# Attention values of one batch by seven products of blocks, in halves of the TensorE array's columns

## The chip, the cores and the metric

The program runs on one core of a Trainium2 chip. The core has five engines that run their own instruction streams and meet through semaphores: TensorE (matrix products, in the profile PE, and PEld for the loading of the stationary operand), VectorE (DVE), ScalarE (ACT), GpSimd (POOL) and SyncE (SP, which here issues the DMAs). The metric is the device time of one execution in microseconds (us), less is better. Three runs of the kernel before took 2408.09 to 2408.88 us, with a median of 2408.5 us.

## What is computed

The input is four images `x` of 512 channels and 32 x 32 places (1024 tokens), float32. Four layers follow each other, each adding its result to `x`: attention with eight heads of 64 channels, a linear attention, attention with one head of 512 channels after a layer norm, and attention with four heads of 128 channels after a group norm. The change is in the last layer, of which this is the core:

```python
attn = jnp.einsum('bhdn,bhdm->bhnm', q, k) / math.sqrt(hd)   # hd = 128, 4 heads
attn = jax.nn.softmax(attn, axis=-1)
out = jnp.einsum('bhnm,bhdm->bhnd', attn, v)
...
return x + conv1x1(out, proj_w, proj_b)
```

## The kernel before

Images are worked off one after another. For each, `project_qkv` makes queries, keys and values, and `attention` (from L917) does the rest. All data are float32, and a float32 matmul shows as two matmul instructions in the trace, each with a weight load of its own.

In the four-head layer a *step* `(qb, g, i)` is one block of 512 queries (`qb`, two of them), one head (`g`, four) and two tiles of 128 keys (`i`, four): 32 steps for an image. Step n of the last image is meant by its number from 0 to 31, so steps 0 to 3 are head (0,0), steps 12 to 15 head (0,3), steps 28 to 31 head (1,3).

- `scores(n)`: two matmuls with a full 128x128 stationary operand and 512 moving columns (L953), into a PSUM tile of two banks, of which there are two. One exponential on ScalarE over 128x1024 (L958) writes the tile `pt`, of which there are four. VectorE keeps the running sum of the head's exponentials (L964 for the second step of a head, L967 after that) and at the head's last step adds the two halves of the sum (L974).
- `values(n)`: two matmuls (L999) that multiply the values of the step's keys with `pt` and add up in one PSUM bank `acc` over the four steps of a head. There are four such banks. At the head's last step ScalarE copies the result to a part of the tile `ot` (L1007); there is one such tile, so the first head of the second query block waits with its copy until the first block has been projected.
- `sum_shared` (L1035): sums over the keys for all heads of a query block in one PSUM bank, with a stationary operand of 128x32 per head; then the reciprocal on VectorE (L693) and two maxima over it that a range check needs (L696), and a round trip by DMA through HBM that spreads the quotients over the partitions (L1047, L1050). In the last image the last head is left out of its block's sharing and has a sum of its own, `sum_rows` (L1024).
- `normalise` (L1068): VectorE multiplies `ot` with the quotients, three ticks after the sums, `issue_after` the newest running sum.
- `project_out` (four ticks after the sums): the output projection of the first block, by seven products of blocks (L1095), with the additions on VectorE (L1103, L1126). It stands in TensorE's stream as one piece of about 12 us.
- `end_program`: for the last query block of the last image; full products (L1146), of which three quarters are done before the last head is normalised, then the result of the range check (L1746 to L1751), the rest, and the output DMAs.

The loop at the end of `attention` writes the order down: iteration m does `scores(m)`, then for step m - 2 the sums if it is a head's last step, and `values(m - 2)`, then a tick for what is due later. TensorE's stream is kept in just this order (a manual schedule). The other engines' instructions are ordered by the framework's scheduler by readiness and priority; `soon()` raises the priority of an exponential, `issue_after` puts an instruction behind a named one.

"Seven products" is a scheme that other parts of the kernel use already: a product of 2 x 2 blocks by seven block products in place of eight, with four sums of weight blocks (`sum_weights`, on GpSimd, L711 to L715) and four sums of input blocks (`sum_inputs`, L701 to L704). Two places use a stationary operand of 64 columns, one in each half of the array's columns: `features(1)` of the linear attention (L1404) and `keys_times_values` (L1529), which also swaps the two halves of the partitions by two DMAs (L1537).

Of the kernel before, what the change touches and what calls it, by code (L numbers as in the profile page):

```python
# [13 lines left out]
F32 = mybir.dt.float32  # L14
AF = mybir.ActivationFunctionType
ALU = mybir.AluOpType
AX = mybir.AxisListType

P = 128
# [3 lines left out]
NC = C // P  # L23
NT = S // P
TB = 512
# [450 lines left out]
def plain_path(ctx: ExitStack, tc: tile.TileContext, d: dict, out: bass.AP, count):  # L476
# [11 lines left out]
    nc = tc.nc  # L488
# [11 lines left out]
    def acc_tile():  # L500
        return ps_acc.tile([P, TB], F32, tag="acc", name="acc")
# [7 lines left out]
    def pt_tile(name):  # L509
        return work.tile([P, 2, TB], F32, tag="pt", bufs=4, name=name)  # L510
# [15 lines left out]
    def chunks_tile(tag, name, bufs=1):  # L526
        return work.tile([P, NC, TB], F32, tag=tag, bufs=bufs, name=name)
# [389 lines left out]
    def attention(b, q, key, v, heads, scale, wo, os, bo, hooks={}, last=False, end=None):  # L917
# [7 lines left out]
        x = xs[b]  # L925
# [14 lines left out]
        group_of = {u: us for us in shared for u in us}  # L940
        parts_of, adds = {}, []

        def scores(n):
            qb, g, i = steps[n]
            ps = two_tile("sc")
            if pair:
                for h, s in itertools.product(range(2), range(2)):
                    nc.tensor.matmul(  # L948
                        ps[half(h), s, :], lhsT=key(g, i)[half(s), half(h)],
                        rhs=q[qb][half(s), g, :], start=True, stop=True,  # L950
                    )
            for s in range(0 if pair else 2):
                nc.tensor.matmul(  # L953
                    ps[:, s, :], lhsT=key(g, 2 * i + s), rhs=q[qb][:, g, :], start=True, stop=True
                )
            pt = pt_tile("pt")
            with soon():
                exps.append(nc.scalar.activation(pt, ps, AF.Exp, scale=scale).ins)  # L958
            pts[n] = pt
            us = group_of.get((qb, g), [])  # L960
            if i == 1:
                acc = many_tile("sum")[:, :2, :] if pair and g % 2 and us else sum_tile("sum")
                accs[qb, g] = acc
                adds.append(nc.vector.tensor_tensor(acc, pts[n - 1], pt, ALU.add).ins)  # L964
            elif i > 1:
                acc = accs[qb, g]
                adds.append(nc.vector.tensor_tensor(acc, acc, pt, ALU.add).ins)  # L967
            if i == nsteps - 1 and not pair:
                total = acc[:, 0, :]
                if us:  # L970
                    if g == 0:
                        parts_of[qb] = many_tile("sums")
                    total = accs[qb, g] = parts_of[qb][:, g, :]
                nc.vector.tensor_tensor(total, acc[:, 0, :], acc[:, 1, :], ALU.add)  # L974

        def values(n):
            qb, g, i = steps[n]
            pt = pts.pop(n)
            if i == 0:
                outs[qb, g] = [acc_tile() for _ in range(2 if pair else 1)]  # L980
# [189 lines left out]

        per = 2 if pair else 1
        parts = []
        for m in range(0, len(steps) + 2, per):
            for n in range(m, m + per):
                if n < len(steps):
                    scores(n)
            for n in range(m, m + per):
                if n >= 2:
                    qb, g, i = steps[n - 2]
                    final = i == nsteps - 1  # L1180

                    us = group_of.get((qb, g))
# [2 lines left out]
                        sum_shared(us)  # L1185
                    elif final and not pair and not us:
                        sum_rows(qb, g)
                    values(n - 2)
                    tick()
                    if final and pair and closes:  # L1190
                        if n - 2 < len(steps) - 1:
                            later.append([1, lambda us=us: sum_shared(us)])
                        else:
                            sum_shared(us)
# [4 lines left out]
                        later.append([3, lambda us=us: normalise_shared(us)])  # L1199
                    elif final and not pair and not us:  # L1200
                        normalise(qb, g)
                    if n - 2 == len(steps) - 1 and end is not None:
                        flush()
                        end_program(qb)
                    elif final and g == NC - 1:
# [828 lines left out]
```

## Time and profile before

The profiled execution took 2407.96 us by the device's clock; the profile's own span is 2406.2 us, the rest lies around it.

| what | us | from |
|---|---|---|
| span | 2406.2 | page |
| profiled execution | 2407.96 | times |
| TensorE matmul busy | 2396.1 | page, part 1 |
| four-head layer, scores (all images) | 239.8 | L953, 512 instructions |
| four-head layer, values (all images) | 240.8 | L999, 512 instructions |
| first scores of the last image start | 2261.13 | timeline |
| first row sums, after the scores of step 17 | 2317.87 | timeline, L1035 |
| `project_out` of the first block | 2334.42 to 2346.5 | timeline, L1095 |
| second row sums | 2372.35 | timeline, L1035 |
| `end_program` starts | 2386.32 | timeline, L1146 |

How to read it: a busy time is the union of an engine's instructions, so two that run side by side count once; the mean is that of one instruction from its start to its end, and on TensorE it holds the way through the array, so matmuls overlap (one of 512 columns lasts 0.59 us and the next starts 0.43 us after it). A weight load starts when the matmul before its own starts. In the timeline an entry in brackets is the time that the engine was idle before the instruction, and what ended it.

### The profile page before, as it was taken

Reading aid. Unit: us, or ns where it says so; the run is one execution under the profiler, and the core shown is the slowest. Engines: PE = TensorE matmul, PEld = TensorE weight load, DVE = VectorE, ACT = ScalarE, POOL = GpSimd, SP = SyncE. Lnnn points to the kernel's source line nnn. Section 1 sums busy time; section 2 is a strip of 40 time slices with the busy share of each in tenths; the row PEclk is TensorE's granted clock in tenths of the full one; section 3 lists DMA queues with packets and bytes.
Section 4 is the critical chain, followed back from the end, with each engine's and each line's share of the span. In section 5 each row is a group of like instructions: output and inputs, shape, how many; then the busy total and the mean of one; then the engine's idle time right before and its main releaser. Section 6 shows DMA issues by size and latency. Waiting matters only on the chain. (4 is left out here: it accounts for less than half of the span.)

```text
span 2406.2 us, 24706 instructions
## 1 busy us (share of the span) xinstructions
PE 2396.1 (100%) x10014; PEld 1197.0 (50%) x10014; DVE 1505.6 (63%) x1834; ACT 702.1 (29%) x866; POOL 245.9 (10%) x240
## 2 busy tenths in 40 slices
PE   9999999999999999999999999999999999999999
PEld 5444544453445344544646445455556446455653
DVE  3678577757875789685585865654563554445344
ACT  1454154315531653230302202013321330331132
POOL 4001100110020001102102021011020001002000
PEclk9999999999999999999999999999999999999999
DMA  6001220212021213111002020110010001000001
GB/s 188 10 10 36 57 80 10 62 31 80 19 62 63 100 37 95 64 66 79 18 9 79 22 87 0 62 70 18 36 70 1 22 31 53 0 35 36 0 25 43
DMA packets 45895, 112.28 MB, mean 47 GB/s; under 512 B 3807, under 2 KB 21215, under 8 KB 42830
## 3 DMA queue, kind: packets, MB, share of 16 engines
q1 hardware_dynamic: 45774, 110.64, 13.7%
q8 instruction: 80, 1.31, 0.2%
q14 instruction: 41, 0.34, 0.0%
HBM read 75.79 MB, written 33.78 MB: 46 GB/s over the span
## 5 line engine op out<-in xcount | busy, mean ns | idle before, releaser
L958 ACT ACTIVATE pt<-sc 128x1024 f32<-128x1024 f32 x384 | 379.6, 1022 | 531.4 <-PE sc L953 303.9
L967 DVE TENSOR_TENSOR sum<-sum,pt 128x1024 f32<-128x1024 f32 x256 | 314.5, 1229 | 160.8 <-ACT pt L958 147.5
L984 PE MATMUL acc<-pt,v 64*64 64x512 f32 x2048 | 245.7, 591 | 0.0
L948 PE MATMUL sc<-q,k 64*64 64x512 f32 x2048 | 243.8, 591 | 1.1 <-ACT pt L958 1.1
L999 PE MATMUL acc<-pt,v 128*128 128x512 f32 x512 | 240.8, 594 | 0.0
L953 PE MATMUL sc<-q,k 128*128 128x512 f32 x512 | 239.8, 593 | 0.0
L724 PE MATMUL acc<-t,ws 128*128 128x512 f32 x384 | 173.9, 593 | 0.0
L711 POOL TENSOR_TENSOR ws<-wqkv 128x256 f32<-128x256 f32 (+1 forms) x40 | 39.2, 981 | 1289.9 <-PE acc L1035 513.3
L964 DVE TENSOR_TENSOR sum<-pt 128x1024 f32<-128x1024 f32 x64 | 78.0, 1219 | 137.0 <-ACT pt L958 137.0
L999 PEld LDWEIGHTS acc<-pt,v 128*128 128x128 f32 x512 | 96.6, 190 | 125.3 <-issue 121.6
L953 PEld LDWEIGHTS sc<-q,k 128*128 128x128 f32 x512 | 96.8, 190 | 116.2 <-issue 92.9
L984 PEld LDWEIGHTS acc<-pt,v 64*64 64x64 f32 x2048 | 76.8, 133 | 143.9 <-issue 141.5
L948 PEld LDWEIGHTS sc<-q,k 64*64 64x64 f32 x2048 | 76.4, 133 | 141.8 <-issue 132.9
L724 PEld LDWEIGHTS acc<-t,ws 128*128 128x128 f32 x384 | 72.7, 190 | 88.1 <-issue 86.3
L763 ACT COPY v<-acc 128x512 f32<-128x512 f32 x24 | 14.1, 586 | 305.1 <-PE acc L849 305.1
L693 DVE RECIPROCAL rd<-acc 128x512 f32<-128x512 f32 (+1 forms) x25 | 83.8, 3353 | 29.1 <-PE acc L1035 29.1
L763 ACT COPY q<-acc 128x512 f32<-128x512 f32 x40 | 23.4, 586 | 221.1 <-PE acc L724 221.1
L849 PE MATMUL acc<-ws,t 128*128 128x256 f32 x384 | 87.1, 380 | 0.0
L1095 PE MATMUL acc<-ot,wo 128*128 128x256 f32 x360 | 85.4, 382 | 1.7 <-DVE ot L1068 1.7
L856 PE MATMUL acc<-q,ln 128*128 128x512 f32 x192 | 86.6, 594 | 0.0
L856 PE MATMUL acc<-qs,w 128*128 128x512 f32 x192 | 86.5, 592 | 0.0
L754 DVE TENSOR_TENSOR v<-acc,v 128x512 f32<-128x512 f32 x72 | 49.7, 690 | 53.1 <-PE acc L849 53.0
(321 smaller groups left out, 3392.6 us busy)
## 6 DMA issues: line engine op xcount, KB each, us to landing
home<-x SPq DMA_DIRECT2D x8, 2048.0 KB
x<-home SPq DMA_DIRECT2D x8, 2048.0 KB
rds<-quotients SPq DMA_DIRECT2D x32, 256.0 KB
squares<-squares SPq DMA_DIRECT2D x32, 256.0 KB
out<-x SPq DMA_DIRECT2D x31, 256.0 KB
rds<-quotients SPq DMA_DIRECT2D x7, 1024.0 KB
x<-in_x SPq DMA_DIRECT2D x3, 2048.0 KB
v<-squares SPq DMA_DIRECT2D x12, 512.0 KB
```

The costliest lines, as they stand in the source:

```text
L693: nc.vector.reciprocal(rd, ps)
L724: nc.tensor.matmul(ps, lhsT=w[:, m, :], rhs=x[:, m, :], start=start, stop=stop, skip_group_check=True)
L849: nc.tensor.matmul(ps[:, bass.ts(r, C // 2)], lhsT=x[:, m, bass.ts(2 * o + r, P)], rhs=w[:, m, :], start=(start and r == 0), stop=stop, sk ...
L856: nc.tensor.matmul(ps, lhsT=x[:, m, bass.ts(o, P)], rhs=w[:, m, :], start=start, stop=stop, skip_group_check=True,)
L948: nc.tensor.matmul(ps[half(h), s, :], lhsT=key(g, i)[half(s), half(h)], rhs=q[qb][half(s), g, :], start=True, stop=True,)
L953: nc.tensor.matmul(ps[:, s, :], lhsT=key(g, 2 * i + s), rhs=q[qb][:, g, :], start=True, stop=True)
L958: exps.append(nc.scalar.activation(pt, ps, AF.Exp, scale=scale).ins)
L964: adds.append(nc.vector.tensor_tensor(acc, pts[n - 1], pt, ALU.add).ins)
L967: adds.append(nc.vector.tensor_tensor(acc, acc, pt, ALU.add).ins)
L984: nc.tensor.matmul(outs[qb, g][r][half(s), :], lhsT=v[i // 2][half(r), i % 2, g * P + s * hd : g * P + (s + 1) * hd], rhs=pt[half(r), s, : ...
L999: nc.tensor.matmul(outs[qb, g][0], lhsT=v[j // 2][:, j % 2, bass.ts(g, P)], rhs=pt[:, s, :], start=(j == 0), stop=(j == NT - 1),)
L1095: nc.tensor.matmul(ps[i][:, bass.ts(o, n)], lhsT=w[:, m, bass.ts(o, P)], rhs=t[:, m, :], start=(start and m + o == 0), stop=(stop and m == ...
```

## The change

In the last image alone, for the six heads between the first and the last, the product of values and exponentials is done by seven products of blocks. The blocks of a pair of steps: output, 2 x 2 blocks of 64 channels by 256 queries; inner, two blocks of 256 keys (one step each). A block product has a stationary operand of 128x64 and 256 moving columns and is written to one half of PSUM's partitions, that is to one half of the array's columns. The products are listed in two rows, `left` and `right`, and issued in turn, one of each: four turns at the first step of a pair, three at the second.

- The sums of value blocks (`vsums`) are made once at the start, eight GpSimd instructions of 128x512. The sums of exponentials (`sum_keys`) are made for each pair of steps: three subtractions of 128x512 on GpSimd (the second needs the first, the third the second), one (t[2]) on VectorE.
- A head has two accumulators. Since products for one output block land in different halves, `seven_values` ends a head with two ScalarE copies (`own` in the new tile `room`, and `ot`), two DMAs that swap the halves of `own`, and five VectorE additions, `issue_after` the newest running sum.
- Exponentials go to a ring of six (`ring`, in the storage of the projection's weights), and values follow their scores by three iterations (`lag`), not two.

```diff
+        lag, ring, by_seven = 2, None, set()
+        if end is not None:
+            lag, by_seven = 3, {(qb, g) for qb, g, i in steps[nsteps:-nsteps:nsteps]}
+            ring = wpool.tile([P, 6, 2, TB], F32, tag="wqkv", name="pts")
+            vsums = [chunks_tile("xn", "vs", 2) for _ in range(2)]
+            for kh in range(2):
+                blocks = [
+                    t.rearrange("p m (g i c) -> p (m g) i c", g=NC, i=2)
+                    for t in v[2 * kh : 2 * kh + 2]
+                ]
+                sum_weights(
+                    [vsums[kh][:, k, :].rearrange("p (r c) -> p r c", r=2 * NC) for k in range(4)],
+                    lambda i, j: blocks[j][:, :, i, :],
+                )
+            room = xpool.tile([P, 2 * NC, TB], F32, tag="x", bufs=2, name="room")
+            tsums = {}
+
+        def sum_keys(n):
+            ts = [pt_tile("t") for _ in range(2)]
+            t = [ts[k // 2][:, k % 2, :].rearrange("p (m q) -> p m q", m=2) for k in range(4)]
+            inputs = lambda j, tb: pts[n - 1 + j][:, :, bass.ts(tb, TB // 2)]
+            nc.gpsimd.tensor_tensor(t[0], inputs(0, 1), inputs(0, 0), ALU.subtract)
+            nc.gpsimd.tensor_tensor(t[1], inputs(1, 1), t[0], ALU.subtract)
+            nc.vector.tensor_tensor(t[2], inputs(1, 1), inputs(0, 1), ALU.subtract)
+            nc.gpsimd.tensor_tensor(t[3], inputs(1, 0), t[1], ALU.subtract)
+            tsums[n - 1] = t
+
+        def seven_values(n):
...
+            left = [(0, 0, raw(0, 0, m), inp(0, 0, m), m == 0, m == 1) for m in range(2)]
+            left += [(1, 0, raw(0, 1, m), inp(1, 0, m), m == 0, m == 1) for m in range(2)]
+            left += [(1, 1, sm(3, m), inp(1, 1, m), False, m == 1) for m in range(2)]
+            left += [(0, 1, sm(0, 0), t[0][:, 0, :], False, True)]
+            right = [(0, 1, sm(0, 1), t[0][:, 1, :], True, True)]
+            right += [(0, 0, sm(1, m), t[1][:, m, :], False, m == 1) for m in range(2)]
+            right += [(1, 1, sm(2, m), t[2][:, m, :], m == 0, m == 1) for m in range(2)]
+            right += [(1, 0, raw(1, 1, m), t[3][:, m, :], False, m == 1) for m in range(2)]
+            part = slice(4, None) if i % 2 else slice(0, 4)
+            for calls in zip(left[part], right[part]):
+                for h, (k, c, lhs, rhs, start, stop) in enumerate(calls):
+                    nc.tensor.matmul(
+                        outs[qb, g][k][half(h), bass.ts(c, TB // 2)], lhsT=lhs, rhs=rhs,
+                        start=(start and kh == 0), stop=(stop and kh == 1), skip_group_check=True,
+                    )
...
+            own, other, both_halves = (room[:, k + a, :] for a in range(3))
+            ps = outs.pop((qb, g))
+            nc.scalar.copy(own, ps[0])
...
+            nc.scalar.copy(o, ps[1])
+            for h in range(2):
+                nc.sync.dma_start(other[half(h)], own[half(1 - h)])
+            with tc.issue_after(adds[-1]):
+                nc.vector.tensor_tensor(both_halves, own, other, ALU.add)
+                early, late = slice(0, TB // 2), slice(TB // 2, TB)
+                add = lambda out, a: nc.vector.tensor_tensor(out, out, a, ALU.add)
+                add(o[:, late], both_halves[:, early])
+                add(o[half(1), early], o[half(1), late])
+                add(o[:, late], both_halves[:, late])
+                add(o[half(0), early], own[half(0), early])
+
         def scores(n):
...
-            pt = pt_tile("pt")
+            pt = pt_tile("pt") if ring is None else ring[:, n % 6, :, :]
...
+            if i % 2 and (qb, g) in by_seven:
+                sum_keys(n)
...
         def values(n):
             qb, g, i = steps[n]
+            if (qb, g) in by_seven:
+                seven_values(n)
+                return
...
-        for m in range(0, len(steps) + 2, per):
+        for m in range(0, len(steps) + lag, per):
...
-                if n >= 2:
-                    qb, g, i = steps[n - 2]
+                if n >= lag:
+                    qb, g, i = steps[n - lag]
...
-                    values(n - 2)
+                    values(n - lag)
                     tick()
```

## The prediction

> **What bounds the kernel now.** I read the page's engine rows first, then busy time by stretch of the last batch.
>
> ```profile
> PE 2396.1 (100%) x10014; PEld 1197.0 (50%) x10014; DVE 1505.6 (63%) x1834; ACT 702.1 (29%) x866; POOL 245.9 (10%) x240
> 2282.00:2316.00 34.00, 34.00 (x80) 15.01 (x79) 11.15 (x11) 11.41 (x12) 0.00 (x0) 1.00 0.00 0
> 2373.00:2392.00 19.00, 19.00 (x48) 8.27 (x46) 16.06 (x17) 5.62 (x8) 0.00 (x0) 1.00 0.11 42
> ```
>
> TensorE is the bound, at full clock. In the attention of the last batch (2261 to 2400 us) it is fed without a gap, VectorE works a third of the time, and GpSimd not at all. At the very end VectorE is busy 16.06 of 19 us, which matters below. So I ask what the change makes of TensorE's own stream, and then whether the new VectorE and GpSimd work is ready in time.
>
> The groups, kept apart by shape, tell whether halves of the columns run side by side. A float32 matmul is two instructions (the values line L999 has 512 for 256 calls).
>
> ```profile
> L654 PE MATMUL feat<-x,block 128*128 128x512 f32 x32 | 14.4, 592 | 0.0
> L1404 PE MATMUL feat<-x,block 128*64 128x512 f32 x64 | 14.6, 598 | 0.0
> ```
>
> Both have the same inputs: 64 half-width instructions take the time of 32 full ones, so two halves do run together. The timeline of weight loads around one such block shows what entering and leaving costs:
>
> ```profile
> 240.81 0.19 PEld L724 LDWEIGHTS acc<-t,ws 128*128 128x128 f32 x1 [0.24 <-issue]
> 241.76 0.20 PEld L1404 LDWEIGHTS feat<-x,block 128*64 128x64 f32 x4 [0.76 <-DVE gate L1423]
> 242.24 0.14 PEld L1404 LDWEIGHTS feat<-x,block 128*64 128x64 f32 x2 [0.29 <-issue]
> ...
> 245.34 0.30 PEld L724 LDWEIGHTS acc<-t,wqkv 128*128 128x128 f32 x2 [0.81 <-issue]
> 245.88 0.19 PEld L724 LDWEIGHTS acc<-t,wqkv 128*128 128x128 f32 x1 [0.24 <-issue]
> ```
>
> In a steady stream a load starts every 0.429 us, one matmul ahead. From 240.81 to 245.88 the stream advances by one old matmul, eight pairs and two new ones, 11 x 0.429 = 4.72; it took 5.07. So one visit to another tile shape costs **0.35 us**: the loads of the new shape wait until the array has run out, both ways. The row sums (128x32 stationary) before the values of step 15 give the same: loads at 2316.92 and 2319.40, 2.48 against 5 x 0.429 = 2.15, so 0.34.
>
> **The change, part by part.**
>
> *Products.* Six of eight heads, two pairs of steps each: 12 pairs. Removed per pair: 4 matmuls of 512 columns, 8 x 0.429 = 3.43 us. Added: 14 half-width matmuls of 256 columns, two at a time, 14 slots. A steady 256-column stream (eight L849 loads at 296.90 in 1.70 us, the last 0.19) has (1.70 - 0.19) / 7 = 0.216 a slot: 3.02 us. Gain 0.41 x 12 = **-4.9 us**, the whole of what the change can bring. Half-width streams of 256 are not in the trace. Bounds: 0.216, and 0.274 if the two half loads of 0.137 (by L1404's median) came one after the other and set the pace, which adds 14 x 12 x 0.058 = 9.7. I take 0.216: at 242.24 two half loads together take 0.14 us, so they overlap and fit under it.
>
> [...]
>
> *Shape changes.* Every values call of the six heads stands between full-width scores: 24 visits x 0.35 = **+8.4**. At the two row sums (steps 15 and 27) values follow in a third shape and share one change, 2 x 0.17 less: **+8.1**. Bounds 7.3 (24 x 0.32, less 0.4) and 8.4.
>
> So TensorE's own stream gets **3.2 us longer**, before any wait.
>
> *Lag of three.* No matmul more. At the start TensorE goes on to the scores of step 3 before any values; it needs the exponential of step 1, which ends at 2265.84, and would get there at 2261.13 + 12 x 0.429 = 2266.28: 0. The ring of six exponentials and the other new tiles take storage whose last readers end with the projection before: 0. At the end one pair of scores fewer stands between step 27 and the close; that is counted below.
>
> *GpSimd.* Eight weight sums at the start, 8 x 1.27 = 10.2 us beside the first head's 13.7; first needed some 20 us in. Then three subtractions of 128x512 per pair, 3.8 us in the 7.2 us that a pair now takes; the first two (2.5 us) are needed some 6 us after their exponential ends. By itself that costs nothing, but GpSimd and VectorE get in each other's way. Where GpSimd meets the running sums of this layer, the timeline shows (start, duration):
>
> ```profile
> 1639.28 1.62 POOL L711 TENSOR_TENSOR os<-wo 128x512 f32<-128x512 f32 x1 [43.68 <-DMA wo<-in_wo]
> ...
> 1640.20 1.78 DVE L967 TENSOR_TENSOR sum<-sum,pt 128x1024 f32<-128x1024 f32 x1 [0.42 <-ACT pt L958]
> ...
> 1640.86 2.25 POOL L714 TENSOR_TENSOR os<-wo 128x512 f32<-128x512 f32 x1
> ...
> 1645.44 1.64 DVE L974 TENSOR_TENSOR sums<-sum 128x512 f32<-128x512 f32 x1
> ```
>
> Alone a GpSimd instruction of this shape takes 1.27 us, a running sum 1.22, the last sum 0.69. From the end of the first GpSimd instruction at 1640.90 to 1647.08, 6.18 us, three of GpSimd and three of VectorE (L967 twice, L974) were done, worth 6.94 alone: they take turns, at 0.89 of the sum. Per head the change has on the two engines: 6 x 1.27 subtractions, running sums 3 x 1.23 + 0.69, two t[2] at 0.69, joins 0.69 + 4 x 0.42: 15.8 alone, **14.0** taking turns, against 4 x 1.715 + 2 x 3.02 + 4 x 0.35 = 14.3 of TensorE. It fits, with nothing to spare.
>
> [...]
>
> *Row sums of the first half.* Step 15's reciprocal (3.35) and two maxima (1.36) come on top. Between the sums and the fourth product of step 18, which needs t[2] of step 19, TensorE has 11.9 us. In written order VectorE does 4.7 + (sums 1.23 + 1.23 + 0.69, joins 2.37, t[2] 0.69, GpSimd's turns 3.8) x 0.89 = 13.6: **+1.7**. Bounds: 0, if t[2] goes ahead of the joins; 4.7, if the half swap's DMAs stand behind the quotients' on SP's queue (issue 1.9 us after the reciprocal) and VectorE waits in the joins for them, with the next running sum queued behind. I take 1.7: at 2376.80 a sum written earlier runs after the reciprocal, so the order goes by readiness.
>
> *ScalarE* gets a second copy per head, 0.59 in 14.3 us, and one exponential of 1.02 per 3.5 us: 0. The swap (two 128 KB DMAs, some 3.6 us from copy to use in the earlier layer, L1534 to L1542) lies beside the next head. Four accumulators of which a head holds two: the other two are free a head earlier: 0.
>
> *The end.*
>
> ```profile
> 2373.52 3.35 DVE L693 RECIPROCAL rd<-acc 96x512 f32<-96x512 f32 x1 [4.92 <-PE acc L1035]
> 2390.50 0.30 DVE L1748 TENSOR_REDUCE row<-ok 128x1 f32<-128x144 f32 x1
> 2391.56 0.09 PEld L1750 LDWEIGHTS acc<-ones,row 128*1 128x1 f32 x2 [0.76 <-DVE row L1748]
> ```
>
> VectorE's chain from the sums of three heads to the verdict ends 0.7 us before TensorE gets there. After the change TensorE has values 27 1.3, changes 0.35, scores 31 1.7, values 28 to 30 5.1, sums 0.9, values 31 1.7, early output 5.15: 16.2. VectorE has reciprocal 3.35, two sums 2.46, maxima 1.34, joins 2.37, total 0.69, three quotients 1.89, reciprocal 3.35, maxima 1.34, quotient 0.68, verdict 0.53: 18.0. **+1.8**; bounds 0 and 4.3 (the swap behind the quotients, 2.5 more).
>
> Sum: -4.9 + 8.1 + 1.7 + 1.8 = **+6.7 us**. The profiled execution took 2407.96 (span 2406.2 and 1.8 around it), 0.54 under the median of 2408.5: 2414.7, or **2415.2** as a median.
>
> **Rivals.**
> - *TensorE alone sets it* (22%): every t and join is in time; +3.2, bounds +2.4 to +4.7: about 2411.7. For it: 6 us of notice for each difference. Against: 14.0 in 14.3.
> - *Port and queue bind* (20%): joins wait for swaps with sums behind them, so both waits stand at their upper ends: 3.2 + 4.7 + 4.3 = +12, 2420.7; were t[2] late by 0.5 us in the other eleven pairs as well, +18, 2426. Half streams paced by serial loads, +9.7, end in the same place. Against: order by readiness.
> - *Not slower* (5%): changing shape is free because the queue fetches the other shape's weights early. Then -4.9 + 1.8 = -3.1, 2405.4; it decides where a visit costs under (4.9 - 1.8) / 24 = 0.13 us. Against: 0.35 and 0.34 in two places.
> - Main case 53%: +4.8 to +10.
>
> **How the numbers follow.** A measurement tells 0.2%, 4.8 us, from nothing. The low end is TensorE alone at its cheapest (2410.9), the high end the port case at its dearest. The main case by itself spans 2413.3 to 2418.5. Slower: main, most of port, some of TensorE alone: 0.75. Same: 0.22. Faster needs -4.8, free shape changes and no wait at all: 0.03.
>
> **What would show it.** Half-width value loads four or three pairs at 0.216, with gaps of about 0.76 and 0.81 us before the first loads of each shape; VectorE and GpSimd instructions lengthened to 1.7 and more; waits of TensorE on VectorE near step 18 and at the last row sum. I am wrong if gaps between shapes are near 0.24, or TensorE waits on GpSimd's differences in every pair.

## The result: 0.5% slower

The changed kernel takes 2420.38 us (median of six runs, 2418.77 to 2422.45), the kernel before 2408.44 in the same session (six runs, 2407.86 to 2408.88). The ratio is 1.005, with a 95% interval of 1.0037 to 1.0063: slower by 0.5%, 11.9 us. The forecast was 2415.2, in a range from 2410.9 to 2426, with 2413.3 to 2418.5 for its main case: the direction held and the time lies in the range, but beyond the main case, which said +6.7. The experiments go after the missing 5.2 us.

The page's engine row, and busy time by stretch of the last batch (us, then busy us and instructions of PE, PEld, DVE, ACT and POOL, the granted clock, DMA share and GB/s):

```profile
PE 2403.8 (99%) x10254; PEld 1200.9 (50%) x10254; DVE 1555.9 (64%) x1876; ACT 705.2 (29%) x872; POOL 322.5 (13%) x284
2284.00:2318.00 34.00, 34.00 (x177) 15.40 (x176) 28.16 (x21) 12.40 (x14) 26.70 (x16) 1.00 0.07 17
2340.00:2350.00 10.00, 6.39 (x31) 5.10 (x28) 9.97 (x14) 1.17 (x2) 1.75 (x1) 1.00 0.13 29
2387.00:2406.00 19.00, 15.80 (x32) 6.12 (x30) 14.35 (x20) 3.47 (x6) 0.00 (x0) 0.91 0.17 56
```

Where VectorE worked 11.15 of 34 us and GpSimd nothing, they now work 28.16 and 26.70, and TensorE is still fed without a gap. It is not fed in two places that had no gap before: around the projection of the first half (6.39 busy of 10) and at the close (15.80 of 19, with a clock of 0.91). The page's chain of work is of no help here, since in both kernels it holds only the last microsecond. TensorE's own waits, from the first scores of the last batch to the end, are four:

```profile
PE acc L1187 <- DVE ot L1160: 2.5, 1, 2.5
PE out L1238 <- DVE ot L1160: 2.3, 1, 2.3
PE acc L1187 <- DVE oi L702: 1.1, 1, 1.1
PE acc L1116 <- DVE sum L1063: 0.9, 1, 0.9
```

All four are on VectorE: for the quotients before the projection (L1187 is its product), for the differences of outputs in it, for the total before the last row sum (L1116), and for the quotients before the early output (L1238).

I measure from the first scores of the last batch to the start of the verdict's matmul, which holds all of the change: before 2261.13 to 2391.56, **130.43 us**; after 2263.17 to 2406.02, **142.85 us**, +12.42. (The profiled execution of after took 2422.45. Of its distance to before 2.04 us lie ahead of this stretch: between 920 and 925 us its clock was granted at 0.66, where before had 1.00, in work that the change does not touch.) A start-to-start ledger of TensorE in that stretch, each block held against its count times the steady slot:

| where | us |
|---|---|
| products, 12 pairs x (3.43 - 3.02) | -4.9 |
| changes of tile shape, 24 visits | +8.2 |
| t[2] at the fourth product of step 18 | +0.1 |
| quotients before the projection | +2.6 |
| differences of outputs in the projection | +1.4 |
| total before the last row sum | +1.1 |
| quotients before the early output | +2.4 |
| clock at half after that wait | +1.8 |
| sum | +12.7 (measured 12.4) |

One visit, by the timeline of weight loads. A load of the left half and one of the right start within 0.01 us of each other, and the next pair follows every 0.21 to 0.22 us (from 2284.13 on):

```profile
2282.91 0.19 PEld L1040 LDWEIGHTS sc<-q,k 128*128 128x128 f32 x1 [0.24 <-issue]
2283.86 0.13 PEld L1000 LDWEIGHTS acc<-pts,v 128*64 128x64 f32 x1 [0.76 <-issue]
2283.87 0.13 PEld L1000 LDWEIGHTS acc<-t,vs 128*64 128x64 f32 x1
...
2285.21 0.14 PEld L1000 LDWEIGHTS acc<-pts,v 128*64 128x64 f32 x1
2285.22 0.14 PEld L1000 LDWEIGHTS acc<-t,vs 128*64 128x64 f32 x1
2285.74 0.30 PEld L1040 LDWEIGHTS sc<-q,k 128*128 128x128 f32 x2 [0.39 <-issue]
```

The gap of 0.76 us before the first half-width load is the one that the forecast had seen at other changes of shape. By the ledger's blocks, a block of scores takes 0.198 us more than its slots when values follow, and a block of values 0.150 more when scores follow: 0.35 a visit, as forecast. The half streams run side by side at the forecast slot. So TensorE's own stream came out as worked, and all of the surplus is waiting and the clock behind a wait.

### The profile page after: what moved, and what is told of

Its sections match the earlier page's. It is cut to its first block, busy times and chain, and to the rows that moved or that the text cites. A ratio compares the mean times of both kernels' runs of the same rounds, so it can differ in the third digit from the quotient of the medians.

```text
span 2420.6 us, 25346 instructions
## 1 busy us (share of the span) xinstructions
PE 2403.8 (99%) x10254; PEld 1200.9 (50%) x10254; DVE 1555.9 (64%) x1876; ACT 705.2 (29%) x872; POOL 322.5 (13%) x284
## 5 line engine op out<-in xcount | busy, mean ns | idle before, releaser
L1045 ACT ACTIVATE pt<-sc 128x1024 f32<-128x1024 f32 x352 | 346.8, 1022 | 452.8 <-PE sc L1040 225.3
L1054 DVE TENSOR_TENSOR sum<-sum,pt 128x1024 f32<-128x1024 f32 x240 | 295.0, 1229 | 134.3 <-ACT pt L1045 121.1
L711 POOL TENSOR_TENSOR ws<-wqkv 128x256 f32<-128x256 f32 (+1 forms) x40 | 39.2, 980 | 1290.5 <-PE acc L1127 513.3
L1091 PE MATMUL acc<-pt,v 128*128 128x512 f32 x384 | 180.6, 594 | 0.0
L1051 DVE TENSOR_TENSOR sum<-pt 128x1024 f32<-128x1024 f32 x56 | 68.4, 1221 | 112.5 <-ACT pt L1045 112.5
L1091 PEld LDWEIGHTS acc<-pt,v 128*128 128x128 f32 x384 | 72.5, 190 | 94.0 <-issue 90.8
L693 DVE RECIPROCAL rd<-acc 128x512 f32<-128x512 f32 (+1 forms) x25 | 83.8, 3353 | 22.6 <-PE acc L1127 21.7
L1187 PE MATMUL acc<-ot,wo 128*128 128x256 f32 x360 | 85.4, 382 | 4.2 <-DVE ot L1160 4.2
L1187 PE MATMUL acc<-oi,os 128*128 128x256 f32 x360 | 83.1, 386 | 1.3 <-DVE oi L702 1.3
```

The costliest lines, as they stand in the source:

```text
L693: nc.vector.reciprocal(rd, ps)
L1091: nc.tensor.matmul(outs[qb, g][0], lhsT=v[j // 2][:, j % 2, bass.ts(g, P)], rhs=pt[:, s, :], start=(j == 0), stop=(j == NT - 1),)
L1187: nc.tensor.matmul(ps[i][:, bass.ts(o, n)], lhsT=w[:, m, bass.ts(o, P)], rhs=t[:, m, :], start=(start and m + o == 0), stop=(stop and m == ...
```

## The experiments

### The lag and the ring alone

The forecast put the lag of three at nothing. This kernel takes from the change the lag and the ring of six exponentials, and does all products as before.

```diff
 lag, ring, by_seven = 2, None, set()
 if end is not None:
-    lag, by_seven = 3, {(qb, g) for qb, g, i in steps[nsteps:-nsteps:nsteps]}
+    lag = 3
     ring = wpool.tile([P, 6, 2, TB], F32, tag="wqkv", name="pts")
...
```

> Only the lag of three iterations and the ring of six exponentials are kept; values, sums and the end of a head are as in the kernel before. Theory: no visit to another tile shape is added and VectorE gets no new work, so 0, 2408.4 us, at most +1 at the close, where one pair of scores fewer stands in TensorE's stream. Rival: the lag itself makes the close late (quotients of three heads behind the last reciprocal in VectorE's order); then some of the 5.4 us that the changed kernel waits at the close stay, +2.5 to +5.4, 2411 to 2414 us.

Measured: 2412.49 us (ten runs, 2410.37 to 2412.73), ratio 1.0015 (1.0005 to 1.0025); the stretch takes 134.58 us, +4.15. The forecast's step is refuted. TensorE has one wait, for quotients at the close. VectorE there, first before, then this kernel (L1068 and L1148 are the quotients, L693 the last reciprocal):

```profile
2382.83 0.69 DVE L974 TENSOR_TENSOR sum<-sum 128x512 f32<-128x512 f32 x1
2383.44 1.89 DVE L1068 TENSOR_TENSOR ot<-ot,rds 128x512 f32<-128x512 f32 x3
2385.24 3.35 DVE L693 RECIPROCAL rd<-acc 128x512 f32<-128x512 f32 x1
```

```profile
2382.47 0.69 DVE L1051 TENSOR_TENSOR sum<-sum 128x512 f32<-128x512 f32 x1
2385.25 3.36 DVE L693 RECIPROCAL rd<-acc 128x512 f32<-128x512 f32 x1 [2.09 <-PE acc L1104]
2388.53 1.82 DVE L1148 TENSOR_TENSOR ot<-ot,rds 128x512 f32<-128x512 f32 x3
```

Before, the three quotients stand ahead of the reciprocal. With the lag of three they stand behind it. In the code they are written three ticks after the block's row sums, and so one iteration ahead of the last head's sum, with either lag. What the longer lag takes away is a block of scores between these two sums: the last row sum starts 11.39 us after the shared ones before (2372.35 and 2383.74), 9.68 us here (2374.51 and 2384.19). The transfer that brings the quotients ended 1.46 us ahead of the last row sum before (2382.28), and 0.49 us behind it here (2384.68), within the 2.09 us for which VectorE is idle. An order by readiness would turn round in just this way; that the scheduler reckoned so is not shown. The early output then waits 2.4 us for the quotients. And TensorE does not come back at full speed:

```profile
2388.00:2390.00 2.00, 0.70 (x1) 0.50 (x2) 2.00 (x4) 0.00 (x0) 0.00 (x0) 0.75 0.00 0
2390.00:2392.00 2.00, 2.00 (x4) 0.68 (x3) 2.00 (x4) 0.00 (x0) 0.00 (x0) 0.50 0.00 0
```

The granted clock is 0.50 after the wait, and about 1.8 us more are lost (4.15 less the wait of 2.37). The ten runs fall into two groups, near 2410.4 to 2411.3 and near 2412.5; the profiled one (2412.55) is of the upper. The mean granted clock is 1.0 in three of the four runs of the lower group and 0.999 in all six of the upper. (In some later sessions the kernel before, too, has runs near 2408.2 and near 2410.3.)

### The change of shape alone

The kernel before, in which the scores of steps 4 to 27 are computed in two halves of the columns (twice the instructions, two at a time), so that values and scores are of two shapes but no sums, joins or lag are added.

```diff
+                if end is not None and 4 <= n < 28:
+                    for h in range(2):
+                        nc.tensor.matmul(
+                            ps[half(h), s, :], lhsT=key(g, 2 * i + s)[:, half(h)],
+                            rhs=q[qb][:, g, :], start=True, stop=True,
+                        )
+                    continue
```

> The kernel before, with the scores of the 24 steps 4 to 27 of the last image made by half-width matmuls (128x64 stationary, two at a time in the halves of the columns, 512 moving columns); values stay full width. Nothing else changes, no engine but TensorE gets other work. Theory: 24 visits to another shape at 0.35 us, less 0.2 to 0.3 at the two row sums, are +8.1 us, 2416.5 us. Rival: the visit costs are hidden behind something or belong to the changed kernel's other waits; then at most +2, 2410 us.

Measured: 2416.57 us (five runs), ratio 1.0037 (1.0023 to 1.0051); the stretch takes 138.60, +8.17, with no wait of TensorE. The price of a visit, taken from two places elsewhere in the trace of before, holds here: 8.17 / 24 = 0.34 us. Of the whole change this is the largest term, and it is larger than all that the products can save.

### The change without most of its sums of exponentials

```diff
-            tsums = {}
+            tsums, kept = {}, []
...
+            if kept:
+                tsums[n - 1] = kept[0]
+                return
             ts = [pt_tile("t") for _ in range(2)]
...
             tsums[n - 1] = t
+            kept.append(t)
```

> The changed kernel, but the sums of exponentials are made for the first pair of steps alone, and every later pair multiplies with that pair's sums: left out are 33 of 36 GpSimd subtractions and 11 of 12 t[2] on VectorE, so the output is not the reference's. TensorE's stream is the same instruction for instruction. Theory (VectorE and GpSimd taking turns make VectorE late): the 4.0 us that TensorE waits before and in the first output projection go to under 0.5, and the close keeps most of its 5.4 us, as the joins stay: 2415.5 to 2417 us. Rival (the order in VectorE's queue, with its waits for the swapped halves, not the sharing): the 4.0 us stay, 2420 us.

Measured: 2417.08 us (five runs), ratio 1.0038; the stretch takes 138.88. The waits at the projection (2.6 and 1.4) are gone, and with them 3.97 us; those at the last row sum and at the early output stay as they were (0.9 and 2.3), and since the 3.97 us are the projection's, so did the 1.8 us behind the latter. The mean granted clock of the profiled execution is 0.999. So the projection waits because of the difference work, on whichever of the two engines, and the close does not.

### The quotients ahead of the last reciprocal

```diff
-            invert(rds[qb, g], ps)
+            with nullcontext() if end is None else tc.issue_after(muls[-1]):
+                invert(rds[qb, g], ps)
...
-            nc.vector.tensor_tensor(o, source, rd, ALU.mult)
+            muls.append(nc.vector.tensor_tensor(o, source, rd, ALU.mult).ins)
```

> The changed kernel, with one order changed on VectorE: the reciprocal of the last head's sum comes after the three quotients of its block (in the kernel before it stood so by itself). Theory: the 2.4 us before the last output goes to under 0.7, and with it the stretch of half clock that follows (1.8 us): -3.5 to -4.2, 2416 to 2417 us; the 4.0 us at the first projection stay. Rival (VectorE simply has too much to do at the close, whatever the order): the wait moves to the verdict, 1.5 to 2 us there, and the gain is under 2 us, 2418.5 us or more.

Measured: 2416.95 us (five runs), ratio 1.0037; the stretch takes 138.63, 4.2 less than after. VectorE at the close, in after and in this kernel (L1160 and L1161 are the quotients):

```profile
2393.66 0.42 DVE L1024 TENSOR_TENSOR ot<-ot,room 128x256 f32<-128x256 f32 x1
2395.02 3.36 DVE L693 RECIPROCAL rd<-acc 128x512 f32<-128x512 f32 x1 [0.95 <-PE acc L1116]
2398.30 1.82 DVE L1160 TENSOR_TENSOR ot<-ot,rds 128x512 f32<-128x512 f32 x3
```

```profile
2392.42 0.42 DVE L1024 TENSOR_TENSOR ot<-ot,room 128x256 f32<-128x256 f32 x1
2392.75 1.89 DVE L1161 TENSOR_TENSOR ot<-ot,rds 128x512 f32<-128x512 f32 x3
2394.56 3.35 DVE L693 RECIPROCAL rd<-acc 128x512 f32<-128x512 f32 x1
```

The wait of 2.4 and the slow stretch of 1.8 behind it are both gone (the mean granted clock of the profiled execution is 1.0, in after 0.998); the verdict, which now has the reciprocal last, is not waited for. It was the order, as in the lag's own run, and not the amount of work.

### Scores in halves too

After, with the scores of steps 8 to 30 in halves of the columns: 21 of the 24 visits no longer change the shape.

```diff
+                if by_seven and 8 <= n < 31:
+                    for h in range(2):
+                        nc.tensor.matmul(
+                            ps[half(h), s, :], lhsT=key(g, 2 * i + s)[:, half(h)],
+                            rhs=q[qb][:, g, :], start=True, stop=True,
+                        )
+                    continue
```

> The changed kernel, with the scores of steps 8 to 30 of the last image made half-width as well, so that TensorE changes shape only at the ends of the six heads, at the two row sums and at the first projection. Theory: the visits' 8.1 us fall to about 1; TensorE's own stream is then 3.8 us shorter than before, 12.9 us per head, and VectorE and GpSimd with 14.0 us by turns become the bound: of the 7 us saved 2 to 4 come back as waits of TensorE for the sums of exponentials and at the projection; 2415.5 to 2418 us. Rival (the visits are the cost and the waits have other causes that stay as they are): 2413 us.

Measured: 2414.78 us (ten runs), ratio 1.0028 (1.0018 to 1.0038), between the two expectations; the stretch takes 136.71, 6.1 less. The visits are indeed free in the timeline of weight loads, the gap before a values block being that of a steady stream:

```profile
2284.11 0.14 PEld L1042 LDWEIGHTS sc<-q,k 128*64 128x64 f32 x2 [0.29 <-issue]
2284.53 0.14 PEld L1000 LDWEIGHTS acc<-pts,vs 128*64 128x64 f32 x1 [0.29 <-issue]
2284.54 0.14 PEld L1000 LDWEIGHTS acc<-t,vs 128*64 128x64 f32 x1
```

Of the 7.1 us that the visits cost, about 1 came back, and not as idle time of TensorE, which is 6.48 us in the stretch in place of 6.80: the clock falls to half twice in this stretch, in place of once (0.50 from 2333 to 2335 us and from 2391 to 2393). With TensorE this much earlier, the waits at the projection are gone, and it waits 3.3 us in the middle of a values block, for a difference that VectorE has behind its joins. The timeline of PE, and that of VectorE with the join (L1024) right ahead of the difference, 1.38 us long for a usual 0.42, and the difference itself at 1.64 for 0.69:

```profile
2333.03 0.69 PE L1000 MATMUL acc<-t,vs 128*64 128x256 f32 x1 [3.29 <-DVE t L969]
```

```profile
2329.92 1.38 DVE L1024 TENSOR_TENSOR ot<-ot 64x256 f32<-64x256 f32 x1
2331.33 1.64 DVE L969 TENSOR_TENSOR t<-pts 128x512 f32<-128x512 f32 x1
```

This is the very place, t[2] of step 19 at the fourth product of step 18, where the forecast had put the wait of after. From 2333 to 2335 us the granted clock is 0.50, from 2335 to 2337 it is 0.80, which costs some 1.4 us more (an estimate, 2 x 0.50 + 2 x 0.20).

### All differences on VectorE

```diff
-            nc.gpsimd.tensor_tensor(t[0], inputs(0, 1), inputs(0, 0), ALU.subtract)
-            nc.gpsimd.tensor_tensor(t[1], inputs(1, 1), t[0], ALU.subtract)
+            nc.vector.tensor_tensor(t[0], inputs(0, 1), inputs(0, 0), ALU.subtract)
+            nc.vector.tensor_tensor(t[1], inputs(1, 1), t[0], ALU.subtract)
...
-            nc.gpsimd.tensor_tensor(t[3], inputs(1, 0), t[1], ALU.subtract)
+            nc.vector.tensor_tensor(t[3], inputs(1, 0), t[1], ALU.subtract)
```

> The changed kernel, with all four differences of exponentials on VectorE; GpSimd makes the eight weight sums at the start and nothing after. VectorE gets 36 more instructions of 0.69, 24.8 us in all. Theory (taking turns is the cost, 14.0 us per head): VectorE alone needs 13.0 of 14.3 us per head, so the waits of 4.0 us before and in the first projection get shorter, 0 to 2.5, and the close stays as it is: 2418 to 2420 us. Rival (volume on VectorE): with 24.8 us more the wait at the projection grows past 5 us, 2421.5 us or more.

Measured: 2417.79 us (four runs), ratio 1.0042 (1.0025 to 1.0059); the stretch takes 140.03, 2.8 less than after. Of these 1.0 lie at the projection: the quotients are in time, the differences of outputs make TensorE wait 2.9 us (2.3 of it idle time), in place of 2.6 and 1.4. The other 1.8 are a half clock that is missing at the close (below). So VectorE is not later for 36 instructions more, worth 25 us, but a little earlier at the projection. (By the forecast's own pieces its work is 12.3 us a head, not the 13.0 of the expectation; either is under TensorE's 14.3.) Busy time from 2262 to 2390 us, first of after, then of this kernel (VectorE is the third entry, GpSimd the fifth):

```profile
2262.00:2390.00 128.00, 124.39 (x563) 60.44 (x562) 102.60 (x93) 43.99 (x52) 75.40 (x43) 1.00 0.10 30
```

```profile
2262.00:2390.00 128.00, 125.50 (x561) 59.84 (x559) 97.46 (x134) 45.36 (x54) 9.04 (x6) 1.00 0.12 36
```

VectorE spends 102.60 us on 93 instructions beside GpSimd, and 97.46 on 134 without it. The groups from 2262 to 2340 us say why; in after:

```profile
L969 DVE TENSOR_TENSOR t<-pts 128x512 f32<-128x512 f32 x8 | 13.0, 1625 | 0.0
L1054 DVE TENSOR_TENSOR sum<-sum,pts 128x1024 f32<-128x1024 f32 x10 | 14.5, 1448 | 4.4 <-ACT pts L1045 4.2
L1051 DVE TENSOR_TENSOR sum<-pts 128x1024 f32<-128x1024 f32 x6 | 11.2, 1873 | 9.6 <-ACT pts L1045 9.6
L1024 DVE TENSOR_TENSOR ot<-ot,room 64x256 f32<-64x256 f32 x3 | 4.2, 1405 | 0.2 <-ACT ot L1018 0.2
L967 POOL TENSOR_TENSOR t<-pts 128x512 f32<-128x512 f32 x9 | 15.6, 1739 | 5.2 <-PE acc L1000 3.6 <-ACT pts L1045 1.6
```

and with all on VectorE:

```profile
L967 DVE TENSOR_TENSOR t<-pts 128x512 f32<-128x512 f32 x9 | 6.2, 687 | 0.6 <-PE acc L1000 0.6
L969 DVE TENSOR_TENSOR t<-pts 128x512 f32<-128x512 f32 x9 | 6.2, 685 | 0.0
```

A subtraction of 128x512 costs 0.69 us on VectorE when GpSimd is quiet. Beside GpSimd the same instruction took 1.63 us in the mean, the first running sum of a head 1.87 and the later ones 1.45, both in place of 1.22, and GpSimd's own 1.74 in place of 1.27 (its first weight sums, L711 and L714, in the same stretch). Without its 36 subtractions, 24.8 us, VectorE's 97.46 would be some 73 (an estimate), and beside GpSimd it spent 102.60 on five instructions fewer: GpSimd takes from VectorE at least as much as VectorE would need to do the work itself, so the second engine adds nothing here.

The close waits as in after (1.1 and 2.4), but here the clock stays at 1.00 behind the wait of 2.3 us (2396 to 2400 us); the last section sets the two side by side.

### Putting the cures together

Five kernels have several cures at once. First, scores in halves, and the quotients ahead of the reciprocal (the two diffs above, together):

> Half-width scores as in the run with these alone, and the last reciprocal after the three quotients. Theory: 3.5 to 4.2 us less than with half-width scores alone: 2412 to 2414.5 us; never under 2408.4, as the waits of the shared sums stay. Rival (waits only move): under 1.5 us less.

Measured: 2410.85 us (ten runs), ratio 1.0009 (0.9999 to 1.0019); the stretch takes 134.03. That is 3.9 us less than with scores in halves alone, by the theory's step, though the time is under its range. The wait of 3.3 us for t[2] stays; the close's order is cured. The mean granted clock of the profiled execution is 0.998, as with scores in halves alone. With all differences on VectorE as well:

> As the last, and all four differences of exponentials on VectorE. TensorE needs 12.9 us per head, VectorE 13.0 and the quotients' 0.7 alone, where the two by turns need 14.7. Theory: 1 to 5 us less than with GpSimd's share: 2408 to 2412 us. Rival (VectorE's volume): more than with GpSimd's share, 2414 us and over.

Measured: 2408.43 us (ten runs), ratio 0.9999 (0.999 to 1.0009); the stretch takes 130.56. The wait for t[2] is gone, and waits at the projection come in its place, so that 1.1 of the 3.5 us between these two kernels are idle time (3.3 less 0.8 and 1.4). That the other 2.4 are the granted clock is the author's estimate: its mean over the profiled execution is 0.998 there and 0.999 here, where it is 1.00 from 2337 to 2341 us. The 12 us are gone, and what is left of waits eats the saving: 0.8 and 1.4 us idle at the projection, 0.9 at the last row sum.

Then two kernels that go for these. In the first GpSimd gets back the differences of the two pairs around VectorE's long reciprocal:

```diff
-            nc.vector.tensor_tensor(t[0], inputs(0, 1), inputs(0, 0), ALU.subtract)
-            nc.vector.tensor_tensor(t[1], inputs(1, 1), t[0], ALU.subtract)
+            eng = nc.gpsimd if n in (17, 19) else nc.vector
+            eng.tensor_tensor(t[0], inputs(0, 1), inputs(0, 0), ALU.subtract)
+            eng.tensor_tensor(t[1], inputs(1, 1), t[0], ALU.subtract)
...
-            nc.vector.tensor_tensor(t[3], inputs(1, 0), t[1], ALU.subtract)
+            eng.tensor_tensor(t[3], inputs(1, 0), t[1], ALU.subtract)
```

> Half-width scores in steps 8 to 30, the quotients ahead of the last reciprocal, and all four differences on VectorE but for the pairs that end in steps 17 and 19, whose t[0], t[1] and t[3] go to GpSimd: there VectorE is in its long reciprocal of the first half, which the traces show running beside GpSimd at its usual 3.35 us. The run with all differences on VectorE took 2408.4; of the first scores to the verdict it spent 130.6 us, with some 3.1 us of TensorE waiting at the projection of the first half and 1.1 at the last row sum. Theory (the projection waits because VectorE is behind after the reciprocal, by the differences queued there): six instructions of 0.7 us, 4.1 us, leave VectorE at that place, the projection's waits fall from 3.1 to between 0 and 1.5, and the time to 2405.5 to 2407.5. Rival (what is late at the projection is the half swap and the joins behind it, whatever VectorE does before): the waits stay at about 3, the time at 2408.4; if GpSimd's instructions lengthen VectorE's there as they do elsewhere, 2409 to 2410.

Measured: 2407.78 us (eleven runs), ratio 0.9996 (0.9987 to 1.0005); the stretch takes 129.83, 0.7 less. The idle time at the projection hardly moved (1.2 and 1.1, in sum 2.27 after 2.28), where the theory promised at most 1.5: it failed. Held against their slots, the blocks there are 0.7 us shorter, which is all of the gain. The time lies between the ranges of theory and rival and speaks for neither. In the second the seventh head keeps its whole products:

```diff
-            lag, by_seven = 3, {(qb, g) for qb, g, i in steps[nsteps:-nsteps:nsteps]}
+            lag, by_seven = 3, {(qb, g) for qb, g, i in steps[nsteps:-2 * nsteps:nsteps]}
...
-                if by_seven and 8 <= n < 31:
+                if by_seven and 8 <= n < 27:
```

> As the run with split differences, but the seventh of the eight heads (the third of the second half) is done with whole products too, so that seven products serve five heads, and half-width scores end with step 26. Given up: two pairs of products, 2 x 0.41 = 0.8 us. Gained: the joins of that head (2.4 us of VectorE) no longer stand ahead of the last row sum, where TensorE waits 1.08 us in the run with six heads. Theory (that wait is the joins'): the wait at the last row sum is gone and the time is within 0.5 us of the run with split differences, 2405.5 to 2407.5. Rival (the wait there is that of the running sums and the total, whatever the joins do): 1.08 stays and the time is 0.8 above that run.

Measured: 2408.18 us (eleven runs), ratio 0.9998 (0.9989 to 1.0007); the stretch takes 129.66. The wait at the last row sum is gone, as it had to be if the joins ahead of the total made it. (The differences of that head are gone too, but the run without most of the sums had left these out and kept the wait.) Two pairs of products less pay for it.

In that kernel's timeline VectorE does, between its last join and the first quotient, the head's total, and then a difference, a running sum and three more differences of the next head. The last kernel puts the quotients, and the differences of outputs after them, ahead of the running sum and the three differences behind it:

```diff
-            sum_inputs(t, inputs)
+            with nullcontext() if end is None else soon():
+                sum_inputs(t, inputs)
...
-                        later.append([3, lambda us=us: normalise_shared(us)])
+                        later.append([2 if by_seven else 3, lambda us=us: normalise_shared(us)])
```

> As the run with five heads, but the quotients of the first half and the differences of its outputs stand ahead of a running sum and three weight differences of the next head on VectorE (written one step earlier and marked as urgent); TensorE's and GpSimd's orders are the same. In the run with five heads TensorE waits 1.15 us before the projection for the quotients and 1.12 in it for the differences of outputs, and VectorE does 1.22 + 3 x 0.60 = 3.0 us of other work between the last join and the first quotient. Theory (the wait is VectorE's order at that place): both waits go, 2.3 us, first scores to verdict from 129.7 to about 127.4 us, and the time to about 2406, under the kernel before by some 2.5 us or 0.1%. Rival (the projection waits for the joins and the half swap before them): the waits stay, 2408.2; or the weight differences, now behind, are late for the products after the projection: the wait moves there, 2407 to 2408.

Measured: 2407.66 us (eleven runs, 2406.82 to 2409.03), ratio 0.9995 (0.9986 to 1.0004); the stretch takes 129.19. TensorE's waits:

```profile
PE acc L1196 <- DVE ou L1227: 0.8, 1, 0.8
PE acc L1196 <- DVE x L1204: 0.6, 1, 0.6
PE acc L1851 <- DVE row L1849: 0.2, 1, 0.2
```

The two waits named in the theory are gone, but it promised 2.3 us and 0.5 came. VectorE still has a backlog there, and the additions of the projection's own results now come late in its place. The verdict (L1851) has begun to wait as well. No version measurably beats the kernel before.

## Why the forecast was right in direction and 5 us short

*Products, -4.9: right.* In steady state a pair of half-width matmuls starts every 0.216 us, as one full-width matmul of 256 columns does in before (0.216): side by side the two halves lose nothing.

*Shape changes, +8.1: right*, 8.17 measured by themselves.

*GpSimd and VectorE taking turns, 14.0 in 14.3 us a head, nothing to spare: right.* In the heads without anything on top TensorE never waits for a difference, and the run with scores in halves, which takes 4 x 0.35 = 1.4 us a head out of TensorE's time, waits 3.3 us for t[2] once the reciprocal is on top. That the factor of 0.89 came out is in part luck, for it was read off a stretch that leaves out 0.70 us of the first running sum and in which VectorE waited 1.71 us for ScalarE. The trace of after gives it again: over two heads, from 2289.10 to 2317.70, at least one of the two engines is busy for 26.08 us, with instructions worth 29.5 by their durations alone (an estimate), 0.89. The rows above agree, with t[2] at 1.63 us for 0.69. That such instructions get longer side by side is shown, on VectorE as on GpSimd (1.74 for 1.27); by what mechanism is not.

*Row sums of the first half, +1.7: mechanism right, place and size wrong.* At the place that the step named after lost 0.1. The backlog was real, but it fell due later: the timeline of VectorE and of GpSimd in after, up to the projection,

```profile
2335.55 0.69 DVE L969 TENSOR_TENSOR t<-pts 128x512 f32<-128x512 f32 x1
2336.16 0.42 DVE L1024 TENSOR_TENSOR ot<-ot,room 128x256 f32<-128x256 f32 x1
2336.50 1.76 DVE L1063 TENSOR_TENSOR sums<-sum 128x512 f32<-128x512 f32 x1
2338.19 2.29 DVE L1051 TENSOR_TENSOR sum<-pts 128x1024 f32<-128x1024 f32 x1
2340.40 0.68 DVE L969 TENSOR_TENSOR t<-pts 128x512 f32<-128x512 f32 x1
2341.00 2.35 DVE L1160 TENSOR_TENSOR ot<-ot,rds 128x512 f32<-128x512 f32 x2
```

```profile
2336.27 1.44 POOL L968 TENSOR_TENSOR t<-pts,t 128x512 f32<-128x512 f32 x1 [1.03 <-DVE t L969]
2337.79 1.60 POOL L970 TENSOR_TENSOR t<-pts,t 128x512 f32<-128x512 f32 x1
2340.45 1.75 POOL L967 TENSOR_TENSOR t<-pts 128x512 f32<-128x512 f32 x1 [1.06 <-PE acc L1000]
```

has VectorE without a gap, its total and running sum drawn out to 1.76 and 2.29 beside GpSimd (0.69 and 1.23 without most of the sums), and the quotients starting at 2341.00, where TensorE's last product before the projection started at 2339.93. The step tested one deadline, t[2] of step 19. The same backlog had two more, the quotients before the projection and the differences of outputs in it, and these were nowhere in the sum: 2.6 + 1.4 = 4.0 us. That the difference work causes them is shown (without most of it both waits vanish). On VectorE alone it costs less, but not nothing: there the projection waits 2.9.

*The end, +1.8: wrong.* The step compared two volumes up to the verdict, 18.0 of VectorE with 16.2 of TensorE. The verdict did not wait. In its place stand 1.1 at the last row sum, because of the joins ahead of the total; 2.4 at the early output; and 1.8 of half clock: 5.3. The last two follow from the order of the next point, not from a volume.

*Lag of three, 0: the step that failed.* It looked at the start, at storage, and at the distance between step 27 and the close, but only for the volumes on both sides: its list for the end keeps VectorE's order of before, the three quotients and then the reciprocal. With a block of scores fewer between the two sums, the last head's reciprocal went ahead of the quotients. The lag's own run shows it as 4.15 us, and moving the reciprocal back recovers 4.2 in the full change. The forecast had said that VectorE's order goes by readiness. In the lag's own run that fits, since the transfer of the quotients ends behind the start of the last row sum. In after it fits less: the transfer ends at 2393.26, and VectorE is idle for 0.95 us, from 2394.07 on, ahead of the reciprocal. By what reckoning the order was fixed stays open.

*The rivals.* The time that came is that of "port and queue bind" (2420.7), but not in the way it had said: no join held VectorE up for a swap while sums stood behind it, and the loads do not pace the half streams (0.137 us a load, 0.216 a pair). No run shows the port of its name, only longer instructions (1.63 us for 0.69). "TensorE alone" fell with the four waits, "not slower" with the 0.35 us per visit. The forecast's range reached past 2418.5 only for the sake of "port and queue bind", so that it holds the measured time is luck. (The upper bound of +4.7 for "TensorE alone" does not follow from the bounds stated, 8.4 - 4.9 = 3.5; nothing rests on it.)

## What to carry to other kernels

Half-width products side by side kept the slot of full-width ones here (0.216 us a pair), and between neighbours of their own shape a visit was free; where they alternated with full-width work, each visit cost 0.35 us. So either give the neighbours the same shape or group the visits. A second elementwise engine can add nothing: here 0.69 us of work on VectorE, done on GpSimd, cost VectorE at least as much in lengthened instructions (t[2] 1.63 us for 0.69). So cost it as time of the first engine. When a loop's lag changes, read the order of every other engine again, and check a backlog against every later deadline, not only the nearest.

## What the runs showed of the hardware

Behind some waits of TensorE of 2.28 to 3.29 us the granted clock fell to 0.50, behind others of 2.28 to 2.49 us it stayed at 1.00. In after it fell behind the wait at the early output:

```profile
2398.00:2400.00 2.00, 1.02 (x2) 0.58 (x3) 2.00 (x4) 0.00 (x0) 0.00 (x0) 0.89 0.00 0
2400.00:2402.00 2.00, 2.00 (x3) 0.67 (x2) 2.00 (x5) 0.00 (x0) 0.00 (x0) 0.50 0.00 0
```

It costs 1.8 us, nearly as much as the wait itself: from the start of the early output to the verdict's matmul TensorE takes 7.04 us (2398.98 to 2406.02), in before 5.24 (2386.32 to 2391.56). All waits of over 2 us in the last batch:

| run, wait before | idle, us | granted clock behind it |
|---|---|---|
| after, early output | 2.28 | 0.50 (2400 to 2402 us) |
| lag alone, early output | 2.37 | 0.50 (2390 to 2392) |
| scores in halves, t[2] | 3.29 | 0.50 (2333 to 2335) |
| scores in halves, early output | 2.28 | 0.50 (2391 to 2393) |
| without most of the sums, early output | 2.3 | mean of the execution 0.999 |
| scores in halves and quotients first, t[2] | 3.3 | mean of the execution 0.998 |
| quotients ahead, projection | 2.5 | mean of the execution 1.0 |
| all differences on VectorE, early output | 2.28 | 1.00 (2396 to 2398) |
| all differences on VectorE, projection | 2.3 | 1.00 (2262 to 2390) |
| after, projection | 2.49 | 1.00 (2343 to 2346) |

The length of the wait does not decide it alone: of three waits of 2.28 us two were followed by 0.50 and one by 1.00. Ahead of the 0.66 from 920 to 925 us in after, TensorE waits 1.67 us for quotients (to 920.21); in before it waits as long at the same place (to 919.70), and the clock stays at 1.00. What decides is not shown.
